# Folding the half chunk of a split-precision output projection into sum B: from one stacked and one 64-row pass to two stacked passes

## The chip, the cores and the metric

The kernel runs on one core of one Trainium2 chip. The metric is device microseconds for one execution, lower is better. The time before is 891.86 us, the median of 3 runs (891.42 to 894.44).

## The reference

Input x is 4 x 1024 x 512 float32. After a layer norm two branches are added to it: a time mix with a linear recurrence over the tokens, and a feed-forward network with GELU. The changed part is the last projection of the time mix, `einsum('bth,ch->btc', out, Wv)`.

```python
def attn(x, mix_k, mix_r, Wk, Wr, Wv, decay, gamma, beta):   # x is already normalized
    xx = concatenate([x[:, 1:2], x[:, :-1]], axis=1) - x
    k = einsum('btc,hc->bth', x + xx * mix_k, Wk)            # 704 hidden channels
    r = einsum('btc,hc->bth', x + xx * mix_r, Wr)
    w = exp(-exp(decay))
    # for each token t:  state = state * w + relu(k_t);  out_t = state * r_t
    out = einsum('bth,ch->btc', out, Wv)
    return layernorm(out) * gamma + beta

xn = layernorm(x)
y = x + attn(xn, ...) + ffn(xn, W0, bias0, W1, bias1)        # ffn: 512 -> 2048 -> 512, erf GELU
```

## The kernel before

**Blocks.** The 4096 tokens are worked through as 8 blocks of 512 (`blocks`, index i). A block is 16 iterations n. In each, `up` makes one 128-channel slice of the FFN's hidden layer (8 matmuls into a bank `pd`, L748), ScalarE turns it into `d` (L758, L763), and `down` multiplies an earlier slice with W1 into the four accumulators `pe` (8 matmuls, L770). One piece of the time mix follows, listed in `pieces`. From block 1 on these are: in iterations 0 to 4 the k products (`three_pass`, 12 matmuls), in 5 and 6 the half chunks (`half_pass`, 8 matmuls), in 7 to 11 the r products, and in 12 to 15 the four output pieces `out_piece`, one for each 128 tokens. In the last block the four output pieces stand two and two in iterations 12 and 13.

**Split precision.** TensorE multiplies in the type fp32r. Blocks 0 and 1 multiply the output projection in plain float32 (L650, L662). From block 2 on (`RAW_OUT = 2`) it is made of several fp32r passes, each operand being split: u is the value with its low 12 bits masked off, the rest is l for the states g and d for the weights Wv. With S = 4096, sum A (bank `oa`) collects u·u and l·(S·d), sum B (bank `ob`) collects (u - S·l)·(u - S·d), and the result is A·(1 + 1/S) - B/S (L703, L704).

**Chunks.** The 704 hidden channels are five chunks of 128 and one half chunk of 64 (`NF` = 5, `HF` = 64). A full chunk takes two matmuls into A (L691) and one into B (L696). The half chunk's high and low terms are stacked into 128 rows, so that one matmul into A is enough (L694, tile `gha`); its term for B has 64 rows (L697, tile `ghb`). An output piece has 17 matmuls. `gated_half` makes the two tiles once a block, `split_wv` the weights' terms once, in block 1.

**Order.** From block 1 on the program order of TensorE and of SyncE's DMA queue is the written one (`manual_schedule`). VectorE, ScalarE and GpSimd get theirs from the planner of the framework, which simulates the program with costs of its own when it is built and issues what is ready, earlier code first. On the chip each engine then runs its list in order. What follows a piece (`after`: L608 and L609 behind `three_pass`, L634 and L635 behind `half_pass`, L703 and L704 behind an output piece) is written behind the next iteration's `up`. The next block's input is turned over by 16 VectorE transposes (L330), written in iterations 6 to 10.

**Buffers.** `pd`, `pa`, `pb`, `ph`, `oa` and `ob` share four PSUM banks (`ps_mm`); a matmul group that begins in a bank waits for the instruction that read the bank's former content. The terms live in 63 SBUF slots with the tag `q`.

Of the kernel before, what the change touches and what calls it, by code (L numbers as in the profile page):

```python
# [14 lines left out]
AF = mybir.ActivationFunctionType  # L15
ALU = mybir.AluOpType
# [6 lines left out]
def time_mix_and_gelu_ffn(  # L23
# [14 lines left out]
    bias1: bass.AP,  # L38
    out: bass.AP,
):  # L40

# [9 lines left out]
    nc = tc.nc  # L53
# [10 lines left out]
    S = 4096.0  # L64
    MASK = -4096

    NF = HID // P
    H0 = NF * P
    HF = P // 2
# [13 lines left out]
    def part(name, dtype=F32R, tag="q", bufs=QS):  # L83
        return wide.tile([P, TB], dtype, tag=tag, name=name, bufs=bufs)

    def temp(name):
        return const.tile([P, TB], F32, tag="s", name=name, bufs=5)
# [4 lines left out]
    def bank(name):  # L92
        return ps_mm.tile([P, TB], F32, tag="mm", name=name)
# [58 lines left out]
    wv_raw, wv = {}, {}  # L152
# [79 lines left out]
    def truncated(raw, name):  # L232
        u = temp(name)
        nc.vector.tensor_scalar(u.bitcast(I32), raw.bitcast(I32), MASK, None, ALU.bitwise_and)  # L234
        return u
# [22 lines left out]
    def split_wv(h):  # L258
        raw = wv_raw[h]
        u = truncated(raw, f"vu_{h}")  # L260
        d = temp(f"vd_{h}")
        nc.vector.tensor_sub(d, raw, u)
        if h < NF:
            wv[h] = [part(f"wv_{h}_{p}") for p in range(3)]
            nc.scalar.copy(wv[h][0], u)
            nc.scalar.activation(wv[h][1], d, AF.Copy, scale=S)
            nc.vector.scalar_tensor_tensor(wv[h][2], d, -S, u, ALU.mult, ALU.add)
        else:
            wv[h] = [part(f"wv_{h}_{p}") for p in range(2)]
            nc.scalar.copy(wv[h][0][:HF], u[:HF])  # L270
            nc.scalar.activation(wv[h][0][HF:], d[HF:], AF.Copy, scale=S)
            nc.vector.scalar_tensor_tensor(
                wv[h][1][:HF], d[:HF], -S, u[:HF], ALU.mult, ALU.add
            )

    def load_kr(j, kind, h):
        terms = [part(f"kr_{j}_{kind}_{h}_{p}", tag="kr", bufs=6) for p in range(3)]
# [210 lines left out]
    gs, ghs, ks = {}, {}, {}  # L488
# [24 lines left out]
    def gated_half(j, st, r):  # L513
        if j >= RAW_OUT:
            g = temp(f"gh_{j}")
            nc.vector.tensor_mul(g[:HF], st[:HF], r)
            u, l = temp(f"gu_{j}"), temp(f"gl_{j}")
            nc.vector.tensor_scalar(
                u[:HF].bitcast(I32), g[:HF].bitcast(I32), MASK, None, ALU.bitwise_and
            )  # L520
            ghs[j] = part(f"gha_{j}"), part(f"ghb_{j}")
            nc.scalar.copy(ghs[j][0][:HF], u[:HF])
            nc.vector.tensor_sub(l[:HF], g[:HF], u[:HF])
            nc.scalar.copy(ghs[j][0][HF:], l[:HF])
            nc.vector.scalar_tensor_tensor(
                ghs[j][1][:HF], l[:HF], -S, u[:HF], ALU.mult, ALU.add
            )
            return

        def tokens(ap, odd):  # L530
            return ap.rearrange("p (s two t) -> p s two t", two=2, t=P)[:, :, odd, :]

        ghs[j] = part(f"gh_{j}", F32)[:, : NS // 2 * P]
        ghs[j] = ghs[j].rearrange("p (s t) -> p s t", t=P)
        for odd in range(2):
            nc.vector.tensor_mul(
                ghs[j][odd * HF : (odd + 1) * HF], tokens(st[:HF], odd), tokens(r, odd)
            )
# [24 lines left out]
    def raw_halves(j, sums):  # L563
        for c in range(NC):
            for q, sum_ in enumerate(sums):
                rows = slice(q * HF, (q + 1) * HF)
                for out_, kind, src in (
                    (sum_[:HF], 0, xks[j, c]),
                    (sum_[HF:], 1, xrs[j, c]),
                ):  # L570
                    nc.tensor.matmul(
                        out_,
                        raw_half[rows, kind, c, :],
                        src[rows],
                        start=(c == 0),
                        stop=(c == NC - 1),
                    )

        def after():
            both = temp(f"kr_{j}")  # L580
            nc.scalar.copy(both, sums[0])
            nc.vector.tensor_add(both, both, sums[1])
            rk, st = temp(f"rk_{j}_{NF}"), temp(f"st_{j}_{NF}")
            nc.scalar.activation(rk[:HF], both[:HF], AF.Relu)
            scanned(j, NF, HF, st, rk)
            gated_half(j, st, both[HF:])

        return after
# [29 lines left out]
    def half_pass(j, kind):  # L618
        xs = xks if kind == 0 else xrs
        w = half_w[kind]  # L620
        pa = bank(f"ph_{j}_{kind}")
        for c in range(NC):
            for p in range(2):
                nc.tensor.matmul(
                    pa,
                    w[:, c].rearrange("p two k -> p (two k)"),
                    xs[j, c][p],
                    start=(c == 0 and p == 0),
                    stop=(c == NC - 1 and p == 1),
                )  # L630

        def after():
            a, y = temp(f"a_{j}_{kind}_{NF}"), temp(f"y_{j}_{kind}_{NF}")
            nc.scalar.copy(a[:HF], pa[HF:])  # L634
            nc.vector.tensor_add(y[:HF], pa[:HF], a[:HF])  # L635
            if kind == 0:
                nc.scalar.activation(y[:HF], y[:HF], AF.Relu)
                ks[j] = temp(f"st_{j}_{NF}")
                scanned(j, NF, HF, ks[j], y)
            else:  # L640
                gated_half(j, ks.pop(j), y[:HF])

        return after
# [26 lines left out]
    def residual(i, s, po):  # L670
        mv = small([P, 1, 2], "mv1", f"mvy_{i}_{s}", 4)
        stats_of(mv, 0, po, f"sty_{i}_{s}")
        rstd = rstd_of(mv[:, :, 1], f"ry_{i}_{s}")
        z = zs[i][:, s, :]
        y = temp(f"o_{i}_{s}") if i < RAW_OUT else po
        nc.vector.scalar_tensor_tensor(
            y, po, mv[:, 0, 0:1], gamma_sb, ALU.subtract, ALU.mult
        )

        def rest():  # L680
            nc.vector.scalar_tensor_tensor(y, y, rstd, beta_sb, ALU.mult, ALU.add)
            nc.vector.tensor_add(z, z, y)

        return rest

    def out_three_pass(i, s):
        cols = slice(s * P, (s + 1) * P)
        pa, pb = bank(f"oa_{i}_{s}"), bank(f"ob_{i}_{s}")
        for h in range(NF):
            for p in range(2):  # L690
                nc.tensor.matmul(  # L691
                    pa, gs[i, h][p][:, cols], wv[h][p], start=(h == 0 and p == 0), stop=False
                )
        nc.tensor.matmul(pa, ghs[i][0][:, cols], wv[NF][0], start=False, stop=True)  # L694
        for h in range(NF):
            nc.tensor.matmul(pb, gs[i, h][2][:, cols], wv[h][2], start=(h == 0), stop=False)  # L696
        nc.tensor.matmul(  # L697
            pb, ghs[i][1][:HF, cols], wv[NF][1][:HF], start=False, stop=True
        )

        def after():
            a, y = temp(f"oa_{i}_{s}"), temp(f"oy_{i}_{s}")
            nc.scalar.activation(a, pa, AF.Copy, scale=1.0 + 1.0 / S)  # L703
            nc.vector.scalar_tensor_tensor(y, pb, -1.0 / S, a, ALU.mult, ALU.add)  # L704
            residual(i, s, y)()

        return after

    def out_piece(i, s):
        if i >= RAW_OUT:  # L710
            return out_three_pass(i, s)
        out_full(i, s)
        if s % 2 == 0:
            return lambda: None
        pair = (s - 1, s)
        out_halves(i, pair)

        def after():
            rests = [residual(i, s, pos.pop(s)) for s in pair]
            for rest in rests:  # L720
                rest()

        return after
# [107 lines left out]
    for i in range(len(blocks)):  # L831
        with tc.manual_schedule(
            engines=engines if i == 0 else {nc.tensor.engine, nc.sync.engine}
        ):
            j = i + 1
# [78 lines left out]
            if i == 1:  # L914
                for g in range(NN // G):
                    put(2 * g, store_w0l, g)
                for h, n in enumerate((3, 6, 8, 9, 10, 11)):
                    put(n, split_wv, h)
# [9 lines left out]
            for n in range(NN):  # L928
# [8 lines left out]
                if gelu:  # L937
                    d = gelu()
# [84 lines left out]
```

## Time and profile before

| | |
|---|---|
| time, median of 3 runs | 891.86 us |
| profiled execution: its own time, its span | 891.54 us, 889.7 us |
| TensorE busy, instructions | 98% of the span, 3760 matmuls |
| VectorE busy | 76% |
| ScalarE busy | 44% |
| GpSimd busy | 8% |
| granted TensorE clock | 0.998 |
| DMA | 195.02 MB, 219 GB/s in the mean |
| output pieces with L697 | 24 (blocks 2 to 7, four each) |

The busy share of TensorE is no measure of useful work here: a matmul's record is longer (some 390 ns) than the distance to the next one, since they are pipelined. What is to be read are the starts: the distance between two matmuls that follow each other, and where it is longer than usual.

### The profile page before, as it was taken

Reading aid. Unit: us, or ns where it says so; the run is one execution under the profiler, and the core shown is the slowest. Engines: PE = TensorE matmul, PEld = TensorE weight load, DVE = VectorE, ACT = ScalarE, POOL = GpSimd, SP = SyncE. Lnnn points to the kernel's source line nnn. Section 1 sums busy time; section 2 is a strip of 40 time slices with the busy share of each in tenths; the row PEclk is TensorE's granted clock in tenths of the full one; section 3 lists DMA queues with packets and bytes.
Section 4 is the critical chain, followed back from the end, with each engine's and each line's share of the span. In section 5 each row is a group of like instructions: output and inputs, shape, how many; then the busy total and the mean of one; then the engine's idle time right before and its main releaser. Section 6 shows DMA issues by size and latency. Waiting matters only on the chain.

```text
span 889.7 us, 11084 instructions
## 1 busy us (share of the span) xinstructions
PE 874.0 (98%) x3760; PEld 683.6 (77%) x3760; DVE 676.6 (76%) x1133; ACT 389.5 (44%) x675; POOL 75.5 (8%) x142
## 2 busy tenths in 40 slices
PE   8999999999999999999999999999999999999997
PEld 8666658876588787887778787787878878788875
DVE  5678876998658879598795978869788697865557
ACT  4855524555144443344434354334534344334331
POOL 1100000001111001000110101100011100100001
PEclk9999999999999999999999999999999999999999
DMA  9579648955486654966549655695655956477641
GB/s 269 211 234 341 225 152 285 314 180 168 166 272 248 213 169 163 329 218 222 188 156 338 204 188 196 194 330 187 212 188 194 323 189 211 158 244 274 232 134 49
DMA packets 100165, 195.02 MB, mean 219 GB/s; under 512 B 10991, under 2 KB 25356, under 8 KB 100108
## 3 DMA queue, kind: packets, MB, share of 16 engines
q1 hardware_dynamic: 100048, 194.29, 64.6%
q8 instruction: 30, 0.49, 0.2%
q14 instruction: 27, 0.22, 0.1%
q10 hardware_dynamic: 60, 0.02, 0.0%
HBM read 165.43 MB, written 28.84 MB: 218 GB/s over the span
## 4 chain that ended last, share of the span: by engine, by line
PE 55%; DVE 19%; DMA 3%; issue 2%; POOL 1%; ACT 0%; SPq 0%; DVEq 0%
PE pd L748 15%; PE pe L770 14%; PE pa L596 9%; DVE xnT L330 6%; PE oa L691 6%; PE pb L374 4%; DMA x<-in_L_attn_x 3%; PE ob L696 3%; PE po L650 2%; DVE stx L304 1%; DVE g L492 1%; DVE y L609 1%; PE ob L697 1%; DVE lr L286 1%; DVE y L635 1%
## 5 line engine op out<-in xcount | busy, mean ns | idle before, releaser
L770 PE MATMUL pe<-w,d 128*128 128x512 f32 x1008 | 249.0, 390 | 0.0
L770 PEld LDWEIGHTS pe<-w,d 128*128 128x128 f32 x1008 | 189.2, 188 | 39.6 <-issue 0.2
L748 PE MATMUL pd<-xf,w0h 128*128 128x512 f32 x512 | 207.7, 406 | 6.5 <-DVE y L635 4.4
L748 PE MATMUL pd<-xf,w0l 128*128 128x512 f32 x512 | 199.8, 390 | 0.0
L758 ACT ACTIVATE d<-pd,late_sb 128x512 f16<-128x512 f32 x128 | 87.5, 684 | 128.9 <-PE pd L748 128.4
L748 PEld LDWEIGHTS pd<-xf,w0h 128*128 128x128 f32 x512 | 96.1, 188 | 42.3 <-issue 10.3
L609 DVE SCALAR_TENSOR_TENSOR y<-pb,a 128x512 f32<-128x512 f32 x70 | 48.2, 689 | 94.0 <-PE pb L374 83.1
L748 PEld LDWEIGHTS pd<-xf,w0l 128*128 128x128 f32 x512 | 96.3, 188 | 20.6 <-issue 1.9
L763 ACT CAST d<-d 128x512 fp32r<-128x512 f16 x128 | 79.4, 620 | 2.6
L330 DVE STREAM_TRANSPOSE xnT<-x 32x512 f32<-32x512 f32 x112 | 78.7, 702 | 2.2
L608 ACT ACTIVATE a<-pa 128x512 f32<-128x512 f32 x70 | 41.6, 595 | 84.8 <-PE pa L596 84.7
L596 PE MATMUL pa<-lk,kr 128*128 128x512 f32 x140 | 54.5, 389 | 0.0
L596 PE MATMUL pa<-hk,kr 128*128 128x512 f32 x140 | 54.5, 389 | 0.0
L611 ACT ACTIVATE y<-y 128x512 f32<-128x512 f32 x35 | 22.1, 633 | 64.1 <-DVE y L609 64.1
L691 PE MATMUL oa<-wv,hg 128*128 128x512 f32 x120 | 46.9, 391 | 0.0
L298 POOL TENSOR_SCALAR ry<-mvy 128x1 f32<-128x1 f32 x32 | 16.9, 529 | 353.1 <-DVE mvy L305 353.1
L691 PE MATMUL oa<-wv,lg 128*128 128x512 f32 x120 | 46.7, 389 | 0.0
L596 PE MATMUL pa<-lr,kr 128*128 128x512 f32 x120 | 46.7, 389 | 0.0
L596 PE MATMUL pa<-hr,kr 128*128 128x512 f32 x120 | 46.7, 389 | 0.0
L285 ACT CAST hk<-uk 128x512 fp32r<-128x512 f32 x28 | 17.4, 622 | 47.5 <-DVE uk L234 47.5
L374 PE MATMUL pb<-mk,kr 128*128 128x512 f32 x140 | 37.4, 389 | 0.0
L650 PE MATMUL po<-wvraw,g 128*128 128x512 f32 x80 | 35.6, 592 | 0.0
(167 smaller groups left out, 1331.6 us busy)
## 6 DMA issues: line engine op xcount, KB each, us to landing
w<-w1d SPq DMA_DIRECT2D x110, 512.0 KB, 3.6
kr<-krd SPq DMA_DIRECT2D x195, 256.0 KB, 5.0
w0l<-w0d SPq DMA_DIRECT2D x96, 256.0 KB, 4.1
x<-in_L_attn_x SPq DMA_DIRECT2D x32, 256.0 KB, 5.8
w1d<-w SPq DMA_DIRECT2D x16, 512.0 KB, 2.9
xres<-in_L_attn_x SPq DMA_DIRECT2D x32, 256.0 KB, 5.0
krd<-wt SPq DMA_DIRECT2D x30, 256.0 KB, 2.8
out<-xres SPq DMA_DIRECT2D x28, 256.0 KB, 5.1
```

The costliest lines, as they stand in the source:

```text
L330: nc.vector.transpose(dst[i * Q : (i + 1) * Q, :, :, j, :], src[j * Q : (j + 1) * Q, :, :, i, :],)
L374: return nc.tensor.matmul(dst, w[:, c, :], src, start=(c == 0), stop=(c == NC - 1))
L596: nc.tensor.matmul(pa, w[p][:, c, :], xs[j, c][p], start=(c == 0 and p == 0), stop=(c == NC - 1 and p == 1),)
L608: nc.scalar.activation(a, pa, AF.Copy, scale=1.0 + 1.0 / S)
L609: nc.vector.scalar_tensor_tensor(y, pb, -1.0 / S, a, ALU.mult, ALU.add)
L650: nc.tensor.matmul(pos[s], gs[i, h][:, s * P : (s + 1) * P], wv_raw[h], start=(h == 0), stop=False,)
L691: nc.tensor.matmul(pa, gs[i, h][p][:, cols], wv[h][p], start=(h == 0 and p == 0), stop=False)
L696: nc.tensor.matmul(pb, gs[i, h][2][:, cols], wv[h][2], start=(h == 0), stop=False)
L748: nc.tensor.matmul(pd, w, xf[c], start=(c == 0 and p == 0), stop=(c == NC - 1 and p == 1),)
L758: nc.scalar.activation(d16, pd, AF.Gelu, bias=b0_sb[:, n : n + 1])
L763: nc.scalar.copy(d, d16)
L770: nc.tensor.matmul(pe[s] if sum_ is None else sum_, d[:, s * P : (s + 1) * P], w1[p][:, cols], start=(n == first and p == 0), stop=(n == e ...
```

## The change

In blocks 2 to 7 the half chunk gives nothing to sum A any more. Both its matmuls go into sum B with the stacked states `gh` = [u; l] (128 rows). The weights are stacked in two ways and multiplied by -S: -S·[u; d] and -S·[d; u]. Together they add -S·(u·u + l·d + u·d + l·u), which L704 divides by -S. Tile `ghb` and the VectorE instruction that made it (L525) are gone, and so is L272 for the weights; the weights' four quarters are four ScalarE activations with a scale. Sum A ends with the full chunks.

```diff
@@ split_wv, the half chunk
             wv[h] = [part(f"wv_{h}_{p}") for p in range(2)]
-            nc.scalar.copy(wv[h][0][:HF], u[:HF])
-            nc.scalar.activation(wv[h][0][HF:], d[HF:], AF.Copy, scale=S)
-            nc.vector.scalar_tensor_tensor(
-                wv[h][1][:HF], d[:HF], -S, u[:HF], ALU.mult, ALU.add
-            )
+            for p, (top, low) in enumerate(((u, d), (d, u))):
+                nc.scalar.activation(wv[h][p][:HF], top[:HF], AF.Copy, scale=-S)
+                nc.scalar.activation(wv[h][p][HF:], low[HF:], AF.Copy, scale=-S)
@@ gated_half
-            ghs[j] = part(f"gha_{j}"), part(f"ghb_{j}")
-            nc.scalar.copy(ghs[j][0][:HF], u[:HF])
+            ghs[j] = part(f"gh_{j}")
+            nc.scalar.copy(ghs[j][:HF], u[:HF])
             nc.vector.tensor_sub(l[:HF], g[:HF], u[:HF])
-            nc.scalar.copy(ghs[j][0][HF:], l[:HF])
-            nc.vector.scalar_tensor_tensor(
-                ghs[j][1][:HF], l[:HF], -S, u[:HF], ALU.mult, ALU.add
-            )
+            nc.scalar.copy(ghs[j][HF:], l[:HF])
@@ out_three_pass
                 nc.tensor.matmul(
-                    pa, gs[i, h][p][:, cols], wv[h][p], start=(h == 0 and p == 0), stop=False
+                    pa,
+                    gs[i, h][p][:, cols],
+                    wv[h][p],
+                    start=(h == 0 and p == 0),
+                    stop=(h == NF - 1 and p == 1),
                 )
-        nc.tensor.matmul(pa, ghs[i][0][:, cols], wv[NF][0], start=False, stop=True)
         for h in range(NF):
             nc.tensor.matmul(pb, gs[i, h][2][:, cols], wv[h][2], start=(h == 0), stop=False)
-        nc.tensor.matmul(
-            pb, ghs[i][1][:HF, cols], wv[NF][1][:HF], start=False, stop=True
-        )
+        for p in range(2):
+            nc.tensor.matmul(pb, ghs[i][:, cols], wv[NF][p], start=False, stop=(p == 1))
```

## The prediction, made before the changed kernel was run

> **What bounds the kernel now.** I read the page first, then the groups by form, then the timeline of TensorE around one output piece, then the waits and the chain that ended last. The page and the groups:
>
> ```profile
> PE 874.0 (98%) x3760; PEld 683.6 (77%) x3760; DVE 676.6 (76%) x1133; ACT 389.5 (44%) x675; POOL 75.5 (8%) x142
> PE 55%; DVE 19%; DMA 3%; issue 2%; POOL 1%; ACT 0%; SPq 0%; DVEq 0%
> L697 PE MATMUL ob<-wv,ghb 64*128 64x512 f32 x24 | 12.0, 498 | 0.0
> L694 PE MATMUL oa<-wv,gha 128*128 128x512 f32 x24 | 9.3, 389 | 0.0
> L697 PEld LDWEIGHTS ob<-wv,ghb 64*128 64x128 f32 x24 | 4.4, 183 | 8.4 <-issue 8.4
> ```
>
> TensorE bounds the kernel, and VectorE sets the end in some stretches. The third line is the odd one: L697 streams the same 512 columns as L694 with half the rows and takes 498 ns, not 389, and ahead of its weight load TensorE's load side idles in all 24 cases. What that costs is not in those durations, but in the starts:
>
> ```profile
> 325.49 0.39 PE L694 MATMUL oa<-wv,gha 128*128 128x512 f32 x1
> 325.71 1.29 PE L696 MATMUL ob<-wv,mg 128*128 128x512 f32 x5
> 326.94 0.50 PE L697 MATMUL ob<-wv,ghb 64*128 64x512 f32 x1
> 327.37 0.50 PE L748 MATMUL pd<-xf,w0h 128*128 128x512 f32 x1
> 327.70 0.39 PE L748 MATMUL pd<-xf,w0l 128*128 128x512 f32 x1
> 327.93 0.39 PE L748 MATMUL pd<-xf,w0h 128*128 128x512 f32 x1
> 326.94 0.18 PEld L697 LDWEIGHTS ob<-wv,ghb 64*128 64x128 f32 x1 [0.35 <-issue]
> 327.37 0.19 PEld L748 LDWEIGHTS pd<-xf,w0h 128*128 128x128 f32 x1 [0.25 <-issue]
> ```
>
> The usual distance is 0.227 us (an iteration of 28 matmuls with `three_pass`, 307.06 to 313.41 in the chain, is 6.35 us). Five L696 should bring L697 at 325.71 + 1.135 = 326.85; it starts at 326.94, 0.09 late. The next distance is 0.43 (0.20 too long), the one after 0.33 (0.10 too long), then 0.23 again. The lost time is 0.09 + 0.20 + 0.10 = 0.40 us by unrounded starts. A second count agrees: from the first L691 at 323.22 to that of the next iteration at 331.10 there are 17 + 8 + 8 = 33 matmuls in 7.88 us; 33 x 0.227 is 7.48. The step from L694's bank to L696's costs nothing, so neither the bank nor the sum matters; what differs is the 64 rows.
>
> **What the Trainium skill says.** "TensorEngine Tiling (Array Packing)", Key Properties: "Mode switching requires drain". A 64-row operand is a row-tiled mode there, so L697 switches in and out. The trace agrees: both of its neighbours' loads wait (0.35 and 0.25 us), and blocks 0 and 1 show it too where L650 goes over to 64-row L662. "TensorE: Matmul & The Clock Gate", step 1 (LDWEIGHTS), says that weight loads are pulled ahead of running matmuls and that their time doesn't depend on the rows; here 128-row loads stand one matmul ahead, L697's starts with its own matmul, and 183 against 188 ns agrees on the length. The same page, on the engine queue depths (Architectural detail), says that ScalarE and VectorE queues are strict FIFO; the trace's L608 at 512.95, stuck behind L524 although its matmuls ended about 506.6, agrees.
>
> **The change part by part.**
> 1. *TensorE, 24 output pieces.* 17 matmuls before, 10 + 5 + 2 = 17 after, all of 128 rows. A 128-row matmul at 0.227 takes L697's place (its own distance in the stream), so the gain is the 0.40 us of switching: 24 x 0.40 = 9.6 us. Bounds: the last two matmuls have the same stationary rows and other moving data, as full chunks have, so I see no extra cost; if only the late start were saved, it would be 24 x 0.09 = 2.2.
> 2. *Does the rest follow?* The queue order of SyncE waits for TensorE all along (input loads are released by pb of `three_pass`), so it moves with it. VectorE in a middle output iteration:
>
> ```profile
> 438.54:446.42 7.88, 7.88 (x35) 6.11 (x34) 6.96 (x13) 2.67 (x5) 1.87 (x4) 1.00 0.61 200
> 442.71 0.69 DVE L704 SCALAR_TENSOR_TENSOR oy<-ob,oa 128x512 f32<-128x512 f32 x1 [0.79 <-PE ob L697]
> ```
>
> It is busy 6.96 us (third pair) and waits 0.79 for TensorE; an iteration of 7.48 still covers it. In iteration 15 it has no idle and ends late, by up to 0.4 more, but idles 0.46, 0.35 and 3.19 us soon after. Cost 0.
> 3. *The end of the program.* From the third output piece of block 7 on the chain runs through VectorE and GpSimd to the last add, so the fourth piece's gain and the after-effects of the third are hidden: 22 x 0.40 + 0.20 = 9.0 us remain of 9.6.
> 4. *L525 leaves VectorE*, 684 ns once a block. It stands on the chain:
>
> ```profile
> 297.52 0.04 DVE xnT L330
> 297.56 0.68 issue
> 298.24 0.68 DVE ghb L525
> 298.94 0.70 DVE xnT L330
> 299.64 0.03 issue
> 299.68 0.70 DVE y L609
> 300.38 0.04 issue
> 300.42 2.11 PE pd L748 x8
> ```
>
> In blocks 2 to 6 `pd` waits here for the bank that L609 reads. The distance is 0.67 to 0.70 instead of 0.227, and the next one 0.34: 0.57 us, five times, 2.9 us in all. If L609 moves up by 0.7 us, this goes. But the planner has interleaved transposes with the half chunk's steps, and put one between L525 and L609, which says that in its plan L609 wasn't ready when L525 ended. Behind L609 one more transpose (300.40) is left. Without L525 the planner most likely takes that one into the hole (0.71 us for 0.68), and L609 stays where it is. So I take 0 and keep 2.9 as the other end; below nothing, one more transpose ahead of L609 costs at most 0.72 x 5 = 3.6. In block 7 no transposes are left and VectorE idles: 0.
> 5. *The longer wait in front, at L635* (distances of 0.89 to 1.96 us ahead of `pd` in blocks 2 to 6), comes before L525 in the order: unchanged.
> 6. *ScalarE, once in block 1.* Four activations for two: 2 x 0.63 = 1.27 us more at 206.8 to 208.7; idles of 1.09 ahead and 1.75 us behind cover it, and `d` is made two iterations ahead. L272 (0.675) leaves VectorE. Both 0; if ScalarE's cover were gone, 1.3 once.
> 7. *L703* waits for sum A, which ends one matmul (0.23) earlier; L704 waits for B: 0. One tile of 63 less a block: no wait for a slot shows in the trace, 0. No DMA is added or moved.
>
> Sum: -9.0. Against the profiled execution's own 891.54 us (span 889.7 and 1.8 around it) that is 882.5. It lies 0.3 below the median of 891.86, within the spread of the runs, and I leave it there.
>
> **The rivals.**
> - *B, the second wait goes as well* (the planner leaves L609 right behind the hole, or ScalarE's order moves): 9.0 + 2.9 = 11.9, 879.6 us. For it: L525 is on the chain. Against: the waiting transpose. 22%.
> - *C, part of the gain is given back.* VectorE's list from the input load to L635 could be the limit. If the load (5.0 to 6.6 us, DMA engines 97 to 99% busy there) did not start earlier with TensorE, the waits at L635 would grow by 1.6 us in blocks 3 to 6, all of what the block ahead saved: 4 x 1.6 = 6.4 back, 888.9 us; half of that, 885.7. Against: the load's issue is released by a matmul, and DMA is at 29 to 61% in the output iterations, so there is no backlog to carry over. 10%.
> - *D, slower.* The planner's new list puts more transposes ahead of L635 or L609 in iterations 5 to 8. Each one more per block costs 5 x 0.72 = 3.6 us. From three (10.8) the gain is gone, four (14.4) give 896.9, slower. For it: the plan is simulated, and its order already costs 1.7 us a block at the two waits (mean distance 1.28 less 0.227, the 0.11 behind it, and 0.57). Against: the edit takes work out of this stretch and touches nothing ahead of L635. 3%.
> - *E, it doesn't do what it says:* the 0.40 us isn't due to 64 rows and stays, about 891.5 us. L662 and the clean step from L694 to L696 speak against. 3%.
>
> **How the numbers follow.** The sum as worked out (A) has 62%: 882.5 us, 881.5 to 883.5. B reaches down to 879, a half of C up to 885.7; with 879.0 to 885.5 under 2 in 10 is left out. A measurement of this kernel can tell about 0.3% (2.7 us) from no change. A, B and nearly all of C are faster by more; the end of C and E give 0.05 for no change, D 0.03 for slower.
>
> **What would show it.** Right: in the timeline, all distances from the last L696 to the next `pd` at 0.227, no "issue" ahead of weight loads in the output pieces, 7.48 us from one output iteration to the next, last matmuls as long as the others (389 ns). For step 4: three transposes in a row ahead of L609 and a distance of about 0.67 still there (A), or L609 directly behind the second and the distance gone (B). For step 3: the end still led by VectorE. Wrong: output iterations well above 7.5 us, a wait for L704 or L727 on TensorE, or distances at L635 beyond the 0.89 to 1.96 us of before.

## The result and the profile after

| | before | changed |
|---|---|---|
| median of the runs made with the prediction's result | 891.86 us (5 runs) | 884.64 us (5 runs, 882.60 to 884.84) |
| ratio, 95% interval | | 0.9912 (0.9889 to 0.9935) |
| median of a later group of runs on one chip | 892.50 us (9 runs) | 882.65 us (4 runs, 882.24 to 883.81) |
| ratio, 95% interval | | 0.9889 (0.9876 to 0.9903) |
| profiled execution: its own time, its span | 891.54, 889.7 us | 882.60, 880.8 us |

The kernel is faster, by 7.2 us in the first comparison and 9.85 in the second. Between the two profiled executions lie 8.9 us; 9.0 were forecast.

The page of the changed kernel, its first lines. The number of matmuls is the same, TensorE's busy time falls by 9.4 us, VectorE has seven instructions fewer (six L525, one L272):

```profile
span 880.8 us, 11076 instructions
PE 864.6 (98%) x3760; PEld 685.5 (78%) x3760; DVE 671.5 (76%) x1126; ACT 389.1 (44%) x677; POOL 73.7 (8%) x142
```

Groups by form (count | busy, mean ns | idle before) and then the timeline of TensorE around the first output piece of block 2 (start, us, instruction), matmuls first and weight loads after them:

```profile
L697 PE MATMUL ob<-wv,gh 128*128 128x512 f32 x48 | 14.8, 389 | 0.0
L697 PEld LDWEIGHTS ob<-wv,gh 128*128 128x128 f32 x48 | 9.0, 188 | 1.9
...
325.93 0.39 PE L687 MATMUL oa<-wv,lg 128*128 128x512 f32 x1
326.16 1.30 PE L695 MATMUL ob<-wv,mg 128*128 128x512 f32 x5
327.29 0.62 PE L697 MATMUL ob<-wv,gh 128*128 128x512 f32 x2
327.75 0.39 PE L746 MATMUL pd<-xf,w0h 128*128 128x512 f32 x1
327.97 0.39 PE L746 MATMUL pd<-xf,w0l 128*128 128x512 f32 x1
327.07 0.41 PEld L697 LDWEIGHTS ob<-wv,gh 128*128 128x128 f32 x2
327.52 0.19 PEld L746 LDWEIGHTS pd<-xf,w0h 128*128 128x128 f32 x1
```

Five L695 at 0.227 us bring L697 at 327.29, two L697 bring `pd` at 327.75, and the next follows 0.22 later: nothing is late. The loads stand one matmul ahead (327.07 for 327.29, 327.52 for 327.75), and no "issue" stands behind them. From the first matmul of an output piece to the second behind it, the 24 pieces take 4.08 us each; before they took 4.48 (4.59 in the two pieces of block 7 that stand right behind another piece: their first distance is 0.33, the last part of that piece's loss).

A table by stage (span of the stretch, then busy us and instructions of TensorE, its loads, VectorE, ScalarE, GpSimd) of one output iteration of block 3, and a VectorE line from the next one:

```profile
436.60:444.08 7.48, 7.48 (x34) 6.19 (x33) 6.96 (x14) 2.84 (x5) 1.87 (x4) 1.00 0.65 210
448.22 0.69 DVE L702 SCALAR_TENSOR_TENSOR oy<-ob,oa 128x512 f32<-128x512 f32 x1 [0.46 <-PE ob L697]
```

The iteration is 7.48 us long, not 7.88. VectorE still has 6.96 us of work in it and still waits for TensorE, 0.46 us here.

The chain that ended last, at the place where L525 stood in block 2:

```profile
297.44 0.69 DVE gl L522
298.12 0.03 issue
298.16 0.70 DVE xnT L329
298.86 0.01 issue
298.87 0.71 DVE xnT L329
299.58 0.01 issue
299.59 0.71 DVE xnT L329
300.30 0.03 issue
300.33 0.70 DVE y L605
301.04 0.04 issue
301.08 2.12 PE pd L746 x8
```

Three transposes in a row stand ahead of the read of `pb` (L609 before, L605 now), and `pd` waits for it as before: the five distances are 0.707 to 0.715 us, where they were 0.668 to 0.703.

### The profile page after: what moved, and what is told of

Its sections match the earlier page's. It is cut to its first block, busy times and chain, and to the rows that moved or that the text cites. A ratio compares the mean times of both kernels' runs of the same rounds, so it can differ in the third digit from the quotient of the medians.

```text
span 880.8 us, 11076 instructions
## 1 busy us (share of the span) xinstructions
PE 864.6 (98%) x3760; PEld 685.5 (78%) x3760; DVE 671.5 (76%) x1126; ACT 389.1 (44%) x677; POOL 73.7 (8%) x142
## 4 chain that ended last, share of the span: by engine, by line
PE 55%; DVE 20%; DMA 3%; issue 2%; POOL 1%; ACT 0%; SPq 0%; DVEq 0%
PE pd L746 15%; PE pe L768 14%; PE pa L592 9%; DVE xnT L329 7%; PE oa L687 6%; PE pb L373 4%; PE ob L695 3%; DMA x<-in_L_attn_x 3%; PE po L646 2%; DVE g L491 1%; DVE y L605 1%; DVE stx L303 1%; PE ob L697 1%; DVE lr L285 1%; DVE y L631 1%
## 5 line engine op out<-in xcount | busy, mean ns | idle before, releaser
L746 PE MATMUL pd<-xf,w0h 128*128 128x512 f32 x512 | 205.2, 401 | 6.0 <-DVE y L631 3.8
L605 DVE SCALAR_TENSOR_TENSOR y<-pb,a 128x512 f32<-128x512 f32 x70 | 48.2, 688 | 96.0 <-PE pb L373 88.1
```

The costliest lines, as they stand in the source:

```text
L746: nc.tensor.matmul(pd, w, xf[c], start=(c == 0 and p == 0), stop=(c == NC - 1 and p == 1),)
```

## The experiments

Times are compared with runs of the kernel before on the same chip. The first four share one group, in which its median was 892.01 us, the last three another, with 892.50. Line numbers move a little from kernel to kernel, so the text goes by tiles where they do.

**e1: only the rows.** The kernel before, its term for sum B padded to 128 rows.

```diff
             ghs[j] = part(f"gha_{j}"), part(f"ghb_{j}")
...
+            nc.scalar.copy(ghs[j][1][HF:], l[:HF])
...
+            nc.scalar.activation(wv[h][1][HF:], d[HF:], AF.Copy, scale=0.0)
...
-            pb, ghs[i][1][:HF, cols], wv[NF][1][:HF], start=False, stop=True
+            pb, ghs[i][1][:, cols], wv[NF][1], start=False, stop=True
```

> The kernel before, with its term for sum B (ghb) padded to 128 rows: the lower 64 rows hold l (one more ScalarE copy a block) against weights of zero; L525 stays. VectorE's program order is that of before, line by line. Theory (64 rows drain TensorE, 0.40 us a piece, nothing else matters): all distances in the output pieces 0.227 us, 9.0 us less than before, 882.5 us, equal to the changed kernel. Rival (L525's removal gives part of the gain): slower than the changed kernel by that part, up to 2.9 us, 885.4. Rival (the edit of sum A or the new weights give it): no gain, 891.5.

Measured: 883.73 us (4 runs), ratio 0.9911 (0.9898 to 0.9924). All 24 output pieces take 4.08 us. The timeline of TensorE:

```profile
327.56 1.29 PE L698 MATMUL ob<-wv,mg 128*128 128x512 f32 x5
328.69 0.39 PE L699 MATMUL ob<-wv,ghb 128*128 128x512 f32 x1
328.92 0.39 PE L750 MATMUL pd<-xf,w0h 128*128 128x512 f32 x1
329.14 0.39 PE L750 MATMUL pd<-xf,w0l 128*128 128x512 f32 x1
```

Sixty-four rows of zero weights, which add nothing to the sum, give the gain of 0.40 us a piece in full: a matmul with more rows is cheaper here than one with fewer. The time falls by 8.3 us, between the 7.2 and 9.85 of the changed kernel. Sum A still has its half chunk, L525 is still there, and the weights are otherwise those of before, so none of these is needed for it. The fold into sum B is one way to fill the rows; these runs don't show that it earns more than the padding. The five waits at the bank of `pb` look different in this kernel (0.28 us ahead of `pd`): the added copy on ScalarE holds up the copy of `pa`, so that TensorE waits for `pa`'s bank one matmul group earlier, 0.29 us each. They moved, they did not go: with the longer distances behind them they take 0.60 us a block in both kernels. ScalarE's timeline:

```profile
299.36 0.62 ACT L525 CAST gha<-gl 64x512 fp32r<-64x512 f32 x1 [0.83 <-DVE gl L524]
299.89 0.61 ACT L529 CAST ghb<-gl 64x512 fp32r<-64x512 f32 x1
300.53 0.60 ACT L610 ACTIVATE a<-pa 128x512 f32<-128x512 f32 x1
```

**e2: only L525 taken away.** The kernel before; the 64-row matmul reads other rows.

```diff
-            ghs[j] = part(f"gha_{j}"), part(f"ghb_{j}")
+            ghs[j] = (part(f"gha_{j}"),)
...
-            nc.vector.scalar_tensor_tensor(
-                ghs[j][1][:HF], l[:HF], -S, u[:HF], ALU.mult, ALU.add
-            )
...
-            pb, ghs[i][1][:HF, cols], wv[NF][1][:HF], start=False, stop=True
+            pb, ghs[i][0][:HF, cols], wv[NF][1][:HF], start=False, stop=True
```

> The kernel before without L525: its 64-row matmul into sum B reads the upper half of gha instead (this leaves out the -S*l in that term). TensorE still switches to 64 rows. Theory (a transpose takes L525's place in VectorE's order, L609 stays late): distances of about 0.7 us ahead of pd at L609 remain, 891.5 us, no gain (0 plus or minus 1). Rival (the second wait goes with L525): 2.9 us less, 888.6.

Measured: 891.92 us (14 runs), ratio 0.9996 (0.9987 to 1.0006). No gain. VectorE's timeline shows the hole filled:

```profile
298.13 0.68 DVE L523 TENSOR_TENSOR gl<-gh,gu 64x512 f32<-64x512 f32 x1
298.85 2.15 DVE L330 STREAM_TRANSPOSE xnT<-x 32x512 f32<-32x512 f32 x3
301.03 0.69 DVE L606 SCALAR_TENSOR_TENSOR y<-pb,a 128x512 f32<-128x512 f32 x1
```

The five distances at this read are 0.69 to 0.73 us. An instruction was taken from the chain that ended last, and the planner put another of nearly the same length (0.71 us for 0.68) in its place.

**e3: the change, with 64 rows again in its last pass.**

```diff
-        for p in range(2):
-            nc.tensor.matmul(pb, ghs[i][:, cols], wv[NF][p], start=False, stop=(p == 1))
+        nc.tensor.matmul(pb, ghs[i][:, cols], wv[NF][0], start=False, stop=False)
+        nc.tensor.matmul(pb, ghs[i][:HF, cols], wv[NF][1][:HF], start=False, stop=True)
```

> The changed kernel, with only the upper 64 rows in its last pass into sum B (this leaves out l*u of the half chunk). Everything else of the change stays. Theory (64 rows alone): distances of 0.32, 0.43 and 0.33 us around that matmul are back, 9.0 us more than the changed kernel, about 891.5 us. Rival (the gain came from taking the half chunk out of sum A or from VectorE): as the changed kernel, 882.5.

Measured: 892.33 us (13 runs), ratio 1.0002 (0.9994 to 1.0010). The gain is gone altogether, though everything else of the change is in. TensorE's timeline, and its load side:

```profile
328.30 0.39 PE L696 MATMUL ob<-wv,gh 128*128 128x512 f32 x1
328.61 0.50 PE L697 MATMUL ob<-wv,gh 64*128 64x512 f32 x1
...
328.61 0.18 PEld L697 LDWEIGHTS ob<-wv,gh 64*128 64x128 f32 x1 [0.35 <-issue]
329.04 0.19 PEld L746 LDWEIGHTS pd<-xf,w0h 128*128 128x128 f32 x1 [0.25 <-issue]
```

By unrounded starts it is 0.32 us to the 64-row matmul and 0.43 behind it, as in the kernel before. With e1 this settles it from both sides.

**e4: two 64-row matmuls in a row.** The kernel before, the last matmul into sum B issued twice.

```diff
-        nc.tensor.matmul(
-            pb, ghs[i][1][:HF, cols], wv[NF][1][:HF], start=False, stop=True
-        )
+        for p in range(2):
+            nc.tensor.matmul(
+                pb, ghs[i][1][:HF, cols], wv[NF][1][:HF], start=False, stop=(p == 1)
+            )
```

> The kernel before with its 64-row matmul into sum B issued twice in a row (the term is added twice). 24 more matmuls of 64 rows, no more switches. Theory (what costs is the switch in and out): the second costs its own distance in the stream, 0.227 us, 24 x 0.227 = 5.4 us more, about 897.0 us. Rival (each 64-row matmul costs, since its weight load isn't pulled ahead): 0.43 us or more between the two, 24 x 0.43 = 10.3 us more, about 901.9; at 0.63, 15 more, 906.6.

Measured: 896.77 us (4 runs), ratio 1.0056 (1.0043 to 1.0069), 4.8 us more than before. TensorE's timeline and its load side:

```profile
325.54 1.29 PE L696 MATMUL ob<-wv,mg 128*128 128x512 f32 x5
326.76 0.73 PE L698 MATMUL ob<-wv,ghb 64*128 64x512 f32 x2
327.42 0.50 PE L749 MATMUL pd<-xf,w0h 128*128 128x512 f32 x1
327.76 0.40 PE L749 MATMUL pd<-xf,w0l 128*128 128x512 f32 x1
326.76 0.29 PEld L698 LDWEIGHTS ob<-wv,ghb 64*128 64x128 f32 x2 [0.35 <-issue]
```

A piece of 18 matmuls takes 4.71 us where 17 took 4.48: the second 64-row matmul adds 0.233 us, little more than one of 128 rows. What costs is going from 128 rows to 64 and back, about 0.40 us for the pair, whether one or two 64-row matmuls lie between. 24 x 0.233 = 5.6 us were added; the median shows 4.8, and the interval reaches from 3.8 to 6.2.

This run also takes the pair apart. The second L698 starts at 327.10, so the four distances from the last L696 to the second L749 are 0.32, 0.34, 0.32 and 0.34 us. So each of the two crossings makes its own distance 0.09 us too long (there the weight load starts with its matmul and not one ahead) and the next one 0.11. In the kernel before, with one 64-row matmul, the 0.11 of the way in and the 0.09 of the way out fall on the same distance, the 0.43. The distance between the two 64-row matmuls, 0.34, is thus neither the 0.227 of the theory nor the 0.43 of the rival; the sum is the theory's. A distance of 0.34 also stands behind each of the ten waits of `pd` for its bank in blocks 2 to 6 of the kernel before (0.335 to 0.341), so in the starts a crossing looks like a short stop of TensorE.

**e5 and e6: the transposes put behind fixed points.** After e2 the planner's order was the likely cause of the remaining waits. In the changed kernel it puts five transposes in a row ahead of the first of the two reads (L631), here in block 2:

```profile
289.76 3.57 DVE L329 STREAM_TRANSPOSE xnT<-x 32x512 f32<-32x512 f32 x5
293.35 0.68 DVE L631 TENSOR_TENSOR y<-ph,a 64x512 f32<-64x512 f32 x1
```

The two kernels that follow are the changed one with most of a block's 16 transposes (14 in e5, 10 in e6) issued behind an instruction that the planner had let them pass. e5:

```diff
@@ half_pass, after
-            nc.vector.tensor_add(y[:HF], pa[:HF], a[:HF])
+            summed = nc.vector.tensor_add(y[:HF], pa[:HF], a[:HF])
+            if kind == 1:
+                state["turn_behind"] = summed.ins
@@ three_pass, after
-            nc.vector.scalar_tensor_tensor(y, pb, -1.0 / S, a, ALU.mult, ALU.add)
+            summed = nc.vector.scalar_tensor_tensor(y, pb, -1.0 / S, a, ALU.mult, ALU.add)
+            if kind == 1 and h == 0:
+                state["turn_behind"] = summed.ins
@@ the loop over the blocks
             def turn(first, end):
-                transposed(state["x"], first, end)
+                if i == 0 or first < 2:
+                    transposed(state["x"], first, end)
+                    return
+                with tc.issue_after(state["turn_behind"]):
+                    transposed(state["x"], first, end)
```

e6 leaves out the point in `half_pass` and has `first < 6` for `first < 2`.

> The changed kernel, with 14 of a block's 16 transposes of the next input issued behind fixed points in VectorE's order: those written in iteration 7 behind the add of the second half_pass, those written later behind the first r product's read of pb. No work is added. Theory (the planner's transposes ahead of these two reads make TensorE wait for their banks, 6.9 us in ten waits of the changed kernel's profile, and 0.11 us behind each): the distances ahead of pd fall to 0.227 and 7 to 8 us go, 875 us. Rival (VectorE is simply full there, and the transposes are missed later): the wait comes back in iterations 9 to 12 or at the next block's products, 880 to 883 us.

> As the kernel with ordered transposes, but with only one fixed point: the ten transposes written in iterations 8 to 10 behind the first r product's read of pb; the add of the second half_pass is left to the planner. Its list has one to two transposes ahead of that add in place of ten. Theory: both waits are gone or nearly so, 875 to 877 us. Rival (VectorE is full there): 880 to 883 us.

> The changed kernel once more, on the same chip as the kernels with ordered transposes, for the ratio between them: 0.991 of the kernel before, 882.6 to 884.8 us, output pieces of 7.48 us an iteration, distances of 0.7 us at the read of pb.

Measured: e5 873.73 us (5 runs), ratio to the kernel before 0.9788 (0.9775 to 0.9801); e6 874.01 (4 runs), 0.9791 (0.9778 to 0.9805); the changed kernel beside them 882.65, 0.9889 (0.9876 to 0.9903). Both are some 9 us faster than the changed kernel. VectorE's timeline of e5 in block 2:

```profile
289.13 0.68 DVE L633 TENSOR_TENSOR y<-ph,a 64x512 f32<-64x512 f32 x1 [0.76 <-ACT a L632]
289.85 0.70 DVE L329 STREAM_TRANSPOSE xnT<-x 32x512 f32<-32x512 f32 x1
...
293.21 0.68 DVE L522 TENSOR_TENSOR gl<-gh,gu 64x512 f32<-64x512 f32 x1
293.92 0.70 DVE L329 STREAM_TRANSPOSE xnT<-x 32x512 f32<-32x512 f32 x1
295.20 0.69 DVE L605 SCALAR_TENSOR_TENSOR y<-pb,a 128x512 f32<-128x512 f32 x1 [0.58 <-ACT a L604]
```

and what TensorE waited for (us in total, times, longest), first the two largest entries of the changed kernel, then the list of e5:

```profile
PE pd L746 <- DVE y L631: 3.8, 5, 1.5
PE pd L746 <- DVE y L605: 2.0, 6, 0.4
...
PE small L448 <- issue: 2.8, 1, 2.8
PE idle L391 <- PEq L1012: 0.8, 1, 0.8
PE pt L415 <- DVE x L307: 0.4, 1, 0.4
PE pd L750 <- DVE y L605: 0.2, 1, 0.2
```

VectorE now waits for its input at the two reads (0.76 and 0.58 us) where TensorE waited for VectorE. From block 2 on no wait of TensorE is left (the last entry lies in block 1). From the first output matmul of one block to that of the next it is 104.27 us in blocks 2 to 6, where the changed kernel took 105.2 to 106.4. In the changed kernel's profile the ten waits and the distances behind them come to 8.0 us too much, and its profiled execution and that of e5 lie 8.05 us apart. VectorE wasn't full; its order was what TensorE waited for.

## Why the prediction was right

1. *TensorE, 24 x 0.40 us.* Right: 4.48 to 4.08 us a piece. e1 and e3 show that the rows alone do it, e4 that the switch is what is paid. What happens inside TensorE at a switch stands in no record; the traces show the late weight load and the 0.20 us at each of the two crossings. The lower bound of 2.2 us did not occur. Rival E, that the time isn't due to the rows, is refuted.
2. *Does the rest follow?* Right: VectorE waits 0.39 and 0.46 us for TensorE in two of the output iterations of block 3, and TensorE has no wait in any output piece.
3. *The end.* Right: from the first output matmul of block 7 to the end the span took 32.40 us before and 31.48 after, 0.92 less; 1.0 was forecast (two pieces of 0.40 and 0.20 of the third). The chain there still runs through VectorE and GpSimd from the third piece on.
4. *L525.* Right at the value taken, 0: three transposes in a row, the wait stays, 0.03 us longer on average. Rival B is refuted by e2, whose interval leaves room for 1.2 us at most.
5. *The wait at L635.* Its place stayed; its size did not repeat: 1.89, 0.41, 1.00, 1.60 and 0.67 us ahead of `pd` where it was 1.96, 0.90, 1.08, 1.15 and 1.30, together 0.8 less. In a second profile of the same changed kernel it was 1.53, 0.74, 0.78, 0.68 and 0.70, another 1.1 less. So this is spread between executions. Rival C, which had these waits grow by 1.6 us in four blocks, is refuted by the sum.
6. *ScalarE's added activations* were not tried by themselves. Up to the first output piece of block 2 the changed kernel's profile is 0.67 us later than before; e2, which has the weights of before, is 1.36 later, so that this says nothing.

The parts add up. Up to the first output matmul of block 2: +0.67; from there to that of block 7: -8.66 (20 pieces of 0.40 are 8.0, the waits 0.7); the rest -0.92. Together 8.9 us of span. That this comes within 0.1 us of the forecast is partly luck: the 0.67 and the 0.7 were not forecast, they cancel, and both are of the size by which executions differ anyway. The 8.0 and the 0.92 are the part that the prediction had worked out.

The forecast of 882.5 us was made against one profiled execution, and met that of the changed kernel (882.60) and the second median (882.65); the first median, 884.64, lies 2.1 higher, above the 881.5 to 883.5 given to the sum though within 879.0 to 885.5. No run tells what set that group of five apart. Rival D, slower by the planner's doing, did not come; its mechanism, though, transposes ahead of the two reads, was at work already in the kernel before (its profile has the same ten waits), and e5 shows on the changed kernel what it costs.

## What to carry to other kernels

In this stream of full matmuls a single one with half the rows was not cheaper but dearer, by 0.40 us. Look at the distances between starts around such a matmul, not at its duration, and pad or stack it to 128 rows, or gather the 64-row ones in one run (two in a row paid the switch once; longer runs were not tried). When an instruction on the longest chain is removed, ask what the scheduler will put into its place: here a transpose filled the hole at once, and the chain kept its length. Where an engine that is busy only three quarters of the time holds up the bounding one, tie its deferrable work behind the reads that free a buffer, before making that work smaller.

## What the runs showed of the hardware

A 64-row matmul behind another of 64 rows cost 0.23 us a piece more, about as much as one of 128 rows; the weight load of the second started 0.23 us ahead of its matmul, as loads do in the rest of the stream. Only the two crossings cost, 0.40 us for the pair, with one matmul between them (the kernel before and e3) or two (e4): at each crossing 0.09 us ahead of the first matmul of the other kind, and 0.11 behind it. And a gain nearly as large as that of the change came from moving work and not from removing any: 14 of the 16 transposes a block, of 0.70 us each, at other places in VectorE's order were worth 8.9 us between the medians of e5 and the changed kernel, 10 of them 8.6 (e6).
